# Eight columns of a transposed x copied by DVE in each step, and the scatter product one step behind, in a graph layer on one core

## The chip, the cores and the metric

The kernel runs on one core of one Trainium2 chip. The metric is the device time of one execution in microseconds (us); each run gives one such time, and runs of this kernel lie within about half a per cent of each other. Engines are named as in the profile: PE is the matrix engine (PEld its weight loads), DVE the vector engine, ACT the scalar engine, POOL the engine that issues the indirect gathers, SP the engine that does nothing here but issue DMAs and read registers for their addresses.

## The reference

One layer of a message-passing network over 12,500 nodes (64 features) and 200,000 edges. Edges are sorted by `dst`; `src` is random.

```python
nodes = node_state[edges].reshape(num_edges, -1)          # x[src], x[dst]: 128 features an edge
gates = ssp(edge_state @ We1 + be1) @ We2 + be2           # ssp(v) = softplus(v) - log 2
gates = gates * (1.0 - sigmoid(5.0 * (edges_distance - 3.5)))
h = ssp(nodes @ Wn1 + bn1) @ Wn2 + bn2
message_sum = zeros_like(node_state).at[edges[:, 1]].add(h * gates)
new_state = node_state + (ssp(message_sum @ Ws1 + bs1) @ Ws2 + bs2)
out = layernorm(x + new_state)
```

Half of the input of `nodes @ Wn1` is a row of x for each edge's `src`, so 200,000 random rows of 256 bytes have to be brought in. The other half and the sum over `dst` touch few nodes at a time, since the edges are sorted.

## The kernel before

The edges are cut into 391 groups (`NG`) of 512. A group is four **slots** of 128 edges (`K = 4`), one edge to a partition in tile `xg` (128 x 4 x 128): columns 0 to 63 of a slot take x[src], columns 64 to 105 a one-hot row that says which of 42 neighbouring nodes (`W = 42`) the edge's `dst` is.

x[src] comes in two ways. Most slots are gathered by POOL, one indirect DMA to a slot (`gather`, L231), into a ring of `AHEAD + BEHIND = 19` tiles `xg`; a gather into a used tile waits until the group that had the tile has been through its scatter product. 47 slots are fetched row by row instead (`fetch`, L257): SP issues 7 and ACT 9 direct DMAs of 256 bytes in each step, at addresses that they have read into registers (L245), so that in some groups POOL has three slots or two in place of four.

A loop in Python (L632) writes out the order of the instructions on each engine, one step to a group, with the layers of neighbouring groups interleaved. In step i:

- POOL gathers group i+14; SP loads the edge features and weights of group i+5 (`load`, L278 and L286).
- PE transposes the four slots of group i+1 (L307, into `tx`), and ACT copies the result to SBUF (`xcopy`, L314).
- PE adds biases (L319, L354), and then does the **scatter product** of group i-2 (`scatter`, L383): messages (128 edges x 128) times the one-hot rows, into 84 free columns of the PSUM tile `z` of group i+1. `behind_by` (L624) chooses the group: i-2 up to 12 steps before the end (`CLOSE`), both i-2 and i-1 at that step, and i-1 after it.
- PE does the first layer of group i+1 (L324 for the edge half, L330 for the node half, which waits for `xcopy`); ACT takes exp and log of it (L341, L344), with three row DMAs issued before, between and after them.
- DVE adds the scatter product to the running sums at the place of the group's first node (`window`, L400, two additions, each at an address in a register that DVE has read at L391).
- PE does the second layer of group i (L361, L366, into `gh`); DVE multiplies it by the cutoff (`hcut`, L375) and by the gate (`message`, L379), finishes the softplus of group i+1 (L349), and makes the one-hot rows of group i+3 (L293).
- In some steps there are pieces of the 25 node blocks of the last layer (L419 to L479), which follow when all edges of a block are summed.

Before the loop a table x @ Wn1[64:] + bn1 is made and written to HBM (L591 to L595). Each engine runs its own instructions in this order; between engines there are semaphores.

Of the kernel before, what the change touches and what calls it, by code (L numbers as in the profile page):

```python
# [42 lines left out]
F32 = mybir.dt.float32  # L43
BF16 = mybir.dt.bfloat16
I32 = mybir.dt.int32
# [12 lines left out]
P = 128  # L58
D = 64
# [8 lines left out]
LOADS = 5  # L68
SPREADS = 5
PREPARE = 5  # L70
BEHIND = 5
CLOSE = 12


BLOCK_STEPS = ((2, 3, 4, 4, 6, 7, 8, 9, 10, 14), (2, 3, 3, 4, 5, 6, 7, 8, 9, 10), (1, 2, 1, 2, 3))
# [2 lines left out]
ROWS_FROM = -1  # L78
READY = (5, 7)
LANDED = 4  # L80
CUTOFF = 5.0
EPS = 1e-5
LN2 = 0.6931471805599453
# [3 lines left out]
def node_blocks(N):  # L87

    first = N % NB
    assert N > NB and first % 2 == 0 and first <= HE  # L90
    sizes = ([first] if first else []) + [NB] * (N // NB)
    return [(sum(sizes[:i]), n) for i, n in enumerate(sizes)]


def block_steps(N, NG):

    steps = []
    for at, n in node_blocks(N):
        share = sqrt(min(1.0, (at + n) / N))
        spread = sqrt(share * (1.0 - share) / (NG * GE))  # L100
        steps.append(ceil(NG * (share + SPREADS * spread)))
    return steps


def slots_by_rows(NG):

    slots = []
    for queue in range(2):
        n = 0
        for g in range(READY[queue], NG - 2):  # L110
            if (g - READY[queue] - ROWS_FROM + 1) * ROWS[queue] >= (n + 1) * P:
                slots.append((queue, g, K - 1 - queue))
                n += 1
    return slots


def row_columns(NG):
# [6 lines left out]
def gnn_resnorm_kernel(ctx: ExitStack, tc: tile.TileContext, a: dict, out: bass.AP, E: int):  # L124
# [57 lines left out]
    be3 = const.tile([PIECES, 2, D], BF16, name="be3")  # L182
    row3 = const.tile([PIECES, 2, K, D], BF16, name="row3")
    rs3 = const.tile([PIECES, K, D], BF16, name="rs3")
    wns = const.tile([DW, REST, 2, 2 * D], F32, name="wns")

    xgs, xrs, eTs = {}, {}, {}
# [30 lines left out]
    def padding(g, k):  # L218
        return g * GE + k % 2 * HE + k // 2 * P >= E

    def gather(g):

        xg = loads.tile([P, K, P], F32, name="xg", bufs=AHEAD + BEHIND)
        xgs[g] = xg
        for k in range(K):
            if (g, k) in by_rows:
                continue
            if padding(g, k):
                nc.vector.memset(xg[:, k, :D], 0.0)
                continue  # L230
            note(("gather", g), nc.gpsimd.indirect_dma_start(  # L231
                out=xg[:, k, :D], out_offset=None, in_=x,
                in_offset=bass.IndirectOffsetOnAxis(ap=src_i[:, g, k : k + 1], axis=0)))
# [4 lines left out]
    def read_rows(i, queue, count):  # L238

        count = min(count, rows_left(queue))  # L240
        while i >= ROWS_FROM and len(row_at[queue]) < count:
            q, p = divmod(fetched[queue] + len(row_at[queue]), READ * P)
            assert p % READ == 0
            at = queue * columns_of[0] + q * READ
            row_at[queue] += nc.values_load_multi_w_load_instructions(  # L245
                rows_i[p // READ : p // READ + 1, at : at + READ], engines=[queues[queue].engine], min_val=0,
                max_val=4 * D * (N - 1), skip_runtime_bounds_check_because="src holds rows of x")[1]
# [23 lines left out]
    bases = {}  # L271

    def load(g):
        old = ("scatter", g - LOADS - 4)
        if g % 2 == 0:
            n = min(2, NG - g)
            both = loads.tile([P, 2, HE], F32, name="eT", bufs=4)
            behind(note(("load", g), nc.sync.dma_start(both[:, :n], a["eT"][:, g : g + n, :])), old)  # L278
            for j in range(n):
                eTs[g + j] = both[:, j]  # L280
            _, at = nc.values_load_multi_w_load_instructions(
                base_i[32:33, 2 * g : 2 * g + 4], engines=[SP], min_val=0, max_val=8 * D * (N - 1),
                skip_runtime_bounds_check_because="they were clamped to these bounds")
            bases[g], bases[g + 1] = at[:2], at[2:]
        for h in range(2):
            behind(note(("load", g), nc.sync.dma_start(  # L286
                wns[D:DW, g % REST, h, :].bitcast(U8),
                table_bytes[:, bass.ds(bases[g][h], 8 * D * W)].rearrange("o (w f) -> (o w) f", w=W))), old)

    xTs, zs, us, ss, ghs, hs, msgs, scs = ({} for _ in range(8))  # L290

# [35 lines left out]
    def layer1_node(g):  # L327
        for h in range(2):
            zn = zs[g][:, h, HE * (1 - h) : HE * (2 - h)]
            nc.tensor.matmul(zn, wns[:, g % REST, h, :], xTs[g][:, h], start=True, stop=True,  # L330
                             skip_group_check=True)

    def z_of(g):
        return zs[g].rearrange("p b e -> p (b e)")[:, : 3 * HE]
# [155 lines left out]
    with tc.manual_schedule():  # L490
# [4 lines left out]
        with tc.tile_pool(name="prep", bufs=1) as prep:  # L495
# [11 lines left out]
            for i in range(3):  # L507
                load_x(i)
            nc.sync.dma_start(rows_i, a["rows"])
            dist = cut.rearrange("p g k -> p (g k)")  # L510
            nc.sync.dma_start(dist, a["dist_l"])
            dst_i = rel.bitcast(I32)
# [2 lines left out]
            for g in range(AHEAD):  # L515
# [12 lines left out]
            nc.scalar.dma_start(consts[:, FIRST:], a["consts"][:, FIRST:])  # L528
            nc.scalar.dma_start(wns[:D].rearrange("f r h o -> f (r h) o"),
                                a["Wn1"][:D, :].rearrange("f (r o) -> f r o", r=1).to_broadcast([D, 2 * REST, 2 * D]))  # L530

            dst_f = dst_h.bitcast(F32)
            nc.vector.tensor_copy(dst_f, dst_h)
# [52 lines left out]
            for i in range(PARTS):  # L586
                for c in range(i * CP, (i + 1) * CP, CP // 2):
                    m = CP // 2
                    ps = z_tile().rearrange("p b (k f) -> p (b k) f", k=K)
                    for k in range(m):  # L590
                        nc.tensor.matmul(ps[:, k, :], xT[:, c + k, :], wnb, start=True, stop=True)  # L591
                    tb = prep.tile([P, m, 2 * D], F32, name="tb", bufs=6)
                    nc.scalar.copy(tb[:, :K, :], ps[:, :K, :])
                    nc.vector.tensor_copy(tb[:, K:, :], ps[:, K:m, :])
                    nc.sync.dma_start(by_node[:, c : c + m], tb)  # L595
                    nc.vector.memset(sums[:, c * P : WIDE if c + m == NCH else (c + m) * P], 0.0)
                if i == 1:
                    nc.vector.tensor_copy(base_i[:1], base_b[:1])
                    nc.vector.tensor_scalar(base_i[32:33], base_b[32:33], float(8 * D), None, OP.mult)
                    nc.vector.tensor_scalar(rows_i, rows_i, float(4 * D), None, OP.mult)  # L600
                    for k in range(2):
                        nc.vector.tensor_copy(be3[:, k, :], rows[:, 0, :])
                    for k in range(K):
                        nc.vector.tensor_copy(row3[:, :, k, :], rows[:, 1:3, :])
                        nc.vector.tensor_copy(rs3[:, k, :], rows[:, 3, :])
                if i == 2:
                    nc.scalar.activation(dist, dist, AF.Sigmoid, bias=steep, scale=-5.0)
                    nc.scalar.preload_act_table_set("natural_log_exp_and_others")
                    nc.vector.tensor_copy(rel, dst_i)
                    for t in range(2):  # L610
                        r = rel[:, :, 2 * t : 2 * t + 2]
                        nc.vector.tensor_sub(r, r, base_b[:, :NH].rearrange("p (g h) -> p g h", h=2))


        with tc.tile_pool(name="finish", bufs=1) as finish:
            blocks = list(zip(node_blocks(N), block_steps(N, NG)))
            last = NG - 1
            parts, begun, complete, rest = {}, None, 0, []

            def at(f, g, *more):  # L620
                if 0 <= g < NG:
                    f(g, *more)

            def behind_by(i):  # L624
                close = last - CLOSE
                return [g for g in ([i - 2] if i <= close else []) + ([i - 1] if i >= close else []) if g >= 0]

            for g in range(LOADS - 1):
                load(g)
# [2 lines left out]
            for i in range(-1, last - 1):  # L632
                now = parts.pop(i, [])
                early = [part for part in now if part.tensor]
                at(load, i + LOADS)
                read_rows(i, 0, ROWS[0])
                fetch(i, 0, ROWS[0])
                if i >= 0:
# [4 lines left out]
                fetch(i, 1, ROWS[1] - 6)  # L643
                layer1_bias(i + 1)
                at(layer2_bias, i)
                for n, g in enumerate(behind_by(i)):
                    scatter(g, zs[i + 1][:, 1, HE + 2 * n * W : HE + 2 * (n + 1) * W])
                layer1_edge(i + 1)
                layer1_node(i + 1)
                exps(i + 1)  # L650
                fetch(i, 1, 3)
                logs(i + 1)
                fetch(i, 1, 3)
                for g in behind_by(i):
                    window(g)
                at(layer2, i)
                for part in early:
                    part.tensor(tx_tile())
# [3 lines left out]
                for part in early:  # L662
                    part.others()
                at(onehot, i + 3)
                for part in now:
                    if not part.tensor:
                        part.others()
# [132 lines left out]
def layouts(inputs):  # L800
# [22 lines left out]
    for queue, columns in enumerate(row_columns(NG)):  # L823
        chosen = [out["src_l"].reshape(P, NG, K)[:, g, k] for q, g, k in slots_by_rows(NG) if q == queue]
        v = padded(np.concatenate(chosen), P * columns, 0).reshape(-1, P, READ)
        rows.append(v.transpose(1, 0, 2).reshape(P, columns))
    out["rows"] = np.ascontiguousarray(np.concatenate(rows, axis=1))
    out["dst_l"] = lanes(dst, dst[-1])
    out["dist_l"] = lanes(dist, 1e6)
    out["dst_h"] = np.ascontiguousarray(padded(dst, NR * P * HE, dst[-1]).reshape(NR, P, HE).transpose(1, 0, 2))  # L830
# [42 lines left out]
```

## Time and profile before

| | |
|---|---|
| median of 3 runs | 2684.91 us (2674.76 to 2686.47) |
| the profiled execution: its time, its span | 2686.47 us, 2684.7 us |
| mean granted PE clock | 0.815 of full speed |
| PE / PEld busy | 84% / 65% of the span |
| DVE / ACT / POOL busy | 39% / 36% / 54% |
| instructions on PE / DVE / ACT / POOL | 11373 / 2767 / 1318 / 1520 |
| first L330 / last L330 | 144.1 us / 2661.8 us from the start |
| moved by DMA | 143.53 MB, 53 GB/s on average |

The span runs from the first to the last instruction; 1.8 us of the execution lie outside it. "Busy" leaves out what a sequencer does by itself: reading registers, issuing DMAs, waiting. The recorded ends of matmuls are modelled, so what PE has finished is read better from who starts because of it. The granted clock switches between full and half speed in stretches of some 3 to 27 us all through the loop.

### The profile page before, as it was taken

To read this page: it belongs to the slowest core of one execution; us is meant where nothing else is said; L and a number is where in the kernel's file an instruction comes from. 1 tells how busy PE (TensorE), PEld (TensorE's weight loads), DVE (VectorE), ACT (ScalarE), POOL (GpSimd) and SP (SyncE) were. 2 spreads that over 40 slices of the span, in tenths; PEclk is the share of its full clock that TensorE was granted. 3 is DMA by queue.
4 is the path that set the end of the run, shared out by engine and by line. 5 is a ranking of instruction groups with operands and counts; after the bars stand their busy time and mean duration, and the time that the engine had idled before them with its cause. 6 is when DMAs were issued, how large, how long until landed. Compare 5 with 4: busy or idle time off the path is not lost.

```text
span 2684.7 us, 47845 instructions
## 1 busy us (share of the span) xinstructions
PE 2243.6 (84%) x11373; PEld 1754.9 (65%) x11373; DVE 1052.4 (39%) x2767; ACT 969.6 (36%) x1318; POOL 1441.8 (54%) x1520
## 2 busy tenths in 40 slices
PE   2489888988888888888889788888888888888897
PEld 1467666766666666666667666666666667666676
DVE  1233333333334333344333443434433443444445
ACT  0133333333333333333333333333334333333344
POOL 7335555555555555555555555555555555555520
PEclk9987788788788778788777888778878887787878
DMA  6222222222222212222222222222222222222210
GB/s 159 82 64 52 48 51 49 48 49 48 49 52 50 49 47 51 51 52 47 52 46 50 51 49 53 53 50 53 51 50 50 50 58 48 54 52 50 52 44 25
DMA packets 150911, 143.53 MB, mean 53 GB/s; under 512 B 51887, under 2 KB 98395, under 8 KB 150626
## 3 DMA queue, kind: packets, MB, share of 16 engines
q1 hardware_dynamic: 94090, 88.26, 11.6%
q0 software_dynamic: 48512, 49.77, 9.5%
q10 hardware_dynamic: 8024, 2.37, 0.4%
q8 instruction: 97, 1.59, 0.2%
q14 instruction: 188, 1.54, 0.2%
HBM read 130.59 MB, written 9.63 MB: 52 GB/s over the span
## 4 chain that ended last, share of the span: by engine, by line
PE 64%; another core or an unknown queue 11%; ACTq 10%; ACT 7%; issue 5%; DVE 1%; DMA 0%; DVEq 0%; SPq 0%
PE z L330 16%; PE gh L366 12%; PE z L383 10%; ACTq L257 10%; PE gh L361 7%; PE tx L307 6%; ACT xT L314 6%; PE z L324 4%; PE gh L354 3%; PE z L319 2%; PE tx L419 1%; PE z L591 1%; ACTq L245 1%; PE tx L450 1%
## 5 line engine op out<-in xcount | busy, mean ns | idle before, releaser
L231 POOL DMA_INDIRECT xg<-in_x,src_i x1516 | 1441.6, 951 | 1144.8 <-PE z L383 353.1
L330 PE MATMUL z<-xT,wns 106*128 106x256 f32 x1564 | 574.1, 503 | 322.9 <-ACT xT L314 309.5
L330 PEld LDWEIGHTS z<-xT,wns 106*128 106x128 f32 x1564 | 361.3, 246 | 486.6 <-ACT xT L314 407.9
L341 ACT ACTIVATE u<-z 128x768 f32<-128x768 f32 x392 | 317.4, 810 | 830.4 <-issue 362.4
L366 PE MATMUL gh<-consts,s 128*128 128x64 f32 x3128 | 493.1, 313 | 0.0
L400 DVE TENSOR_TENSOR sums<-sums,z 64x42 f32 x778 | 153.0, 197 | 863.4 <-issue 626.8
L366 PEld LDWEIGHTS gh<-consts,s 128*128 128x128 f32 x3128 | 490.2, 238 | 0.1
L314 ACT COPY xT<-tx 106x512 f32<-106x512 f32 x391 | 228.9, 586 | 670.9 <-remote 231.5
L375 DVE TENSOR_TENSOR h<-gh,cut 128x256 f32<-128x256 f32 x391 | 166.1, 425 | 618.2 <-PE z L383 239.7
L344 ACT ACTIVATE u<-u,one 128x768 f32<-128x768 f32 x392 | 365.9, 934 | 69.7 <-issue 53.3
L349 DVE SCALAR_TENSOR_TENSOR s<-u,z 128x768 f32<-128x768 f32 x392 | 369.4, 943 | 11.1 <-ACT u L344 9.8
L361 PEld LDWEIGHTS gh<-consts,s 128*128 128x128 f32 x1564 | 304.0, 247 | 70.1 <-DVE s L349 32.8
L383 PEld LDWEIGHTS z<-xg,msg 128*128 128x128 f32 x1556 | 240.3, 221 | 152.8 <-issue 148.5
L361 PE MATMUL gh<-consts,s 128*128 128x128 f32 x1564 | 313.8, 335 | 1.8 <-DVE s L349 1.8
L383 PE MATMUL z<-xg,msg 128*128 128x84 f32 x1556 | 306.2, 327 | 0.9 <-DVE msg L379 0.2
L324 PE MATMUL z<-eT,consts 128*128 128x256 f32 x782 | 295.4, 465 | 0.0
L307 PE MATMUL tx<-consts,xg 128*106 128x128 f32 x1517 | 278.6, 312 | 6.4 <-DMA wns<-table 6.4
L307 PEld LDWEIGHTS tx<-consts,xg 128*106 128x106 f32 x1517 | 216.0, 169 | 10.6 <-issue 8.0
L379 DVE TENSOR_TENSOR msg<-gh,h 128x256 f32<-128x256 f32 x391 | 166.0, 425 | 13.4
L354 PE MATMUL gh<-row,ones 3*128 3x512 bf16 x391 | 170.0, 435 | 0.0
L324 PEld LDWEIGHTS z<-eT,consts 128*128 128x128 f32 x782 | 141.7, 226 | 1.2 <-issue 1.2
L293 DVE TENSOR_TENSOR xg<-consts,rel 128x168 f32<-128x168 f32 x391 | 129.9, 332 | 0.0
(93 smaller groups left out, 609.5 us busy)
## 6 DMA issues: line engine op xcount, KB each, us to landing
xr<-in_x ACTq DMA_DIRECT2D x3328, 0.2 KB
eT<-in_eT SPq DMA_DIRECT2D x195, 256.0 KB
xr<-in_x SPq DMA_DIRECT2D x2688, 0.2 KB
xg<-in_x,src_i POOLq DMA_INDIRECT x1516
wns<-table SPq DMA_DIRECT2D x782, 21.0 KB
table<-tb SPq DMA_DIRECT2D x14, 448.0 KB
sums<-in_xT SPq DMA_DIRECT2D x7, 455.0 KB
y<-in_x SPq DMA_DIRECT2D x24, 128.0 KB
```

The costliest lines, as they stand in the source:

```text
L231: note(("gather", g), nc.gpsimd.indirect_dma_start(out=xg[:, k, :D], out_offset=None, in_=x, in_offset=bass.IndirectOffsetOnAxis(ap=src_i[ ...
L257: ins = queues[queue].dma_start(row_tiles[n, "in"][r : r + 1, :D].bitcast(U8), x_bytes[:, bass.ds(row_at[queue].pop(0), 4 * D)])
L307: ins = nc.tensor.transpose(tx[:, k, :], xgs[g][:, k, :DW], ident)
L314: note(("xcopy", g), nc.scalar.copy(xT, xTs[g]))
L324: nc.tensor.matmul(zs[g][:, 0, :HE], we1.rearrange("a h d -> a (h d)"), eTs[g], start=False, stop=True, skip_group_check=True)
L330: nc.tensor.matmul(zn, wns[:, g % REST, h, :], xTs[g][:, h], start=True, stop=True, skip_group_check=True)
L341: nc.scalar.activation(us[g][:, part], z_of(g)[:, part], AF.Exp)
L344: nc.scalar.activation(us[g][:, part], us[g][:, part], AF.Ln, bias=one)
L349: nc.vector.scalar_tensor_tensor(ss[g].rearrange("p i t e -> p (i t e)")[:, part], us[g][:, part], BIG, z_of(g)[:, part], OP.min, OP.max)
L361: nc.tensor.matmul(v[:, 0, t], ss[g][:, 0, t, :], we2, start=False, stop=False, skip_group_check=True)
L366: nc.tensor.matmul(ghs[g][:, 1, 2 * t + h, :], ss[g][:, 1 + h, t, :], wn2, start=False, stop=h == 1 and t == 1, skip_group_check=True)
L383: ins = nc.tensor.matmul(sc, msgs[g][:, 2 * t : 2 * t + 2, :].rearrange("p h f -> p (h f)"), xgs[g][:, 2 * t : 2 * t + 2, D:DW], start=t = ...
```

## The change

Two things are changed together.

**The scatter product.** `behind_by` and `CLOSE` go. In every step the product of group i-1 is made, and added to the sums, in place of that of group i-2. `BEHIND` goes from 5 to 4, so the ring of `xg` has 18 tiles. The condition on `load` moves along: it waits for the scatter of group g-8 in place of g-9, which is the same step.

**The columns.** 23 slots, all with k = 1 (`slots_by_columns`), are no longer gathered by POOL; their columns 0 to 63 of `xg` are set to zero by DVE. The two halves of x lie transposed in SBUF, 64 partitions each, in a tile `xh` of 128 x 6250 float32 (3.2 MB, loaded by SP in four parts in steps 0 to 3). From step 8 on, after the one-hot rows, DVE reads eight indices from SBUF into registers and copies eight columns of `xh` (128 x 1 each) into a tile `column`. 16 steps make one slot, 368 steps all of them. When a slot is full, one instruction sets to zero the half of each column that is another node's (`sides`, `border`), and PE adds Wn1[:64], stacked twice, times that tile to the group's first layer: one 128 x 128 product more in 23 steps. All four transposes of such a group stay.

```diff
-BEHIND = 5
-CLOSE = 12
+BEHIND = 4
+COLUMNS = 8
+COLUMNS_FROM = 8
+XH_PARTS = 4
...
-            if padding(g, k):
+            if padding(g, k) or (g, k) in by_columns:
                 nc.vector.memset(xg[:, k, :D], 0.0)
                 continue
...
+    def columns(i, pool):
+        n = columns_done[0]
+        if i < COLUMNS_FROM or n >= len(by_columns) * P:
+            return
+        p, q = (n // COLUMNS) % P, n // (COLUMNS * P) * COLUMNS
+        _, at = nc.values_load_multi_w_load_instructions(
+            columns_i[p : p + 1, q : q + COLUMNS], engines=[DVE], min_val=0, max_val=half_n - 1,
+            skip_runtime_bounds_check_because="src holds rows of x")
+        slot = list(by_columns)[n // P]
+        if n % P == 0:
+            column_tiles[slot] = pool.tile([P, P], F32, name="column", bufs=2)
+        for j in range(COLUMNS):
+            nc.vector.tensor_copy(column_tiles[slot][:, n % P + j : n % P + j + 1], xh[:, bass.ds(at[j], 1)])
+        columns_done[0] += COLUMNS
+        if columns_done[0] % P == 0:
+            chosen_columns[slot] = pool.tile([P, P], F32, name="chosen", bufs=2)
+            nc.vector.scalar_tensor_tensor(chosen_columns[slot], sides[:, n // P * P : (n // P + 1) * P], border,
+                                           column_tiles[slot], OP.is_ge, OP.mult)
...
+            for t in chosen:
+                nc.tensor.matmul(zn[:, t * P : (t + 1) * P], wn1_twice, chosen_columns[g, 2 * t + h], start=False,
+                                 stop=True, skip_group_check=True)
...
+            nc.sync.dma_start(columns_i, a["columns"])
+            nc.sync.dma_start(sides_i, a["sides"].partition_broadcast(P))
...
+                if 0 <= i < XH_PARTS:
+                    part = slice(half_n * i // XH_PARTS, half_n * (i + 1) // XH_PARTS)
+                    nc.sync.dma_start(xh[:, part], a["xh"][:, part])
...
-                for n, g in enumerate(behind_by(i)):
-                    scatter(g, zs[i + 1][:, 1, HE + 2 * n * W : HE + 2 * (n + 1) * W])
+                if i >= 1:
+                    scatter(i - 1, zs[i + 1][:, 1, HE : HE + 2 * W])
...
-                for g in behind_by(i):
-                    window(g)
+                at(window, i - 1)
...
                 at(onehot, i + 3)
+                columns(i, finish)
```

Ahead of the loop there are also two small loads of Wn1, four DVE instructions that split the indices into a half and a place in it, and a load of 1.5 MB (`sides`, one row sent to all partitions).

More of the change, by code (lines that the diff above doesn't have):

```diff
@@ L114, in slots_by_rows, with slots_by_columns, column_columns @@
     return slots
+def slots_by_columns(NG):
+    slots = []
+    for g in range(NG - 2):
+        if (g - 3 - COLUMNS_FROM + 1) * COLUMNS >= (len(slots) + 1) * P:
+            slots.append((g, 1))
+    return slots
+def column_columns(NG):
+    return -(-len(slots_by_columns(NG)) // COLUMNS) * COLUMNS
 def row_columns(NG):
@@ L184, in gnn_resnorm_kernel @@
     rs3 = const.tile([PIECES, K, D], BF16, name="rs3")
+    half_n = a["xh"].shape[1]
+    by_columns = {slot: n for n, slot in enumerate(slots_by_columns(NG))}
+    columns_i = const.tile([P, column_columns(NG)], I32, name="columns_i")
+    sides_i = const.tile([P, len(by_columns) * P], I32, name="sides_i")
+    sides = sides_i.bitcast(F32)
+    sign = const.tile([P, 1], F32, name="sign")
+    border = const.tile([P, 1], F32, name="border")
+    wn1_twice = const.tile([P, 2 * D], F32, name="wn1_twice")
     wns = const.tile([DW, REST, 2, 2 * D], F32, name="wns")
@@ L273, in load @@
     def load(g):
-        old = ("scatter", g - LOADS - 4)
+        old = ("scatter", g - LOADS - 3)
         if g % 2 == 0:
@@ L288, in load @@
                 table_bytes[:, bass.ds(bases[g][h], 8 * D * W)].rearrange("o (w f) -> (o w) f", w=W))), old)
+    column_tiles, chosen_columns, columns_done = {}, {}, [0]
+    def columns(i, pool):
[16 more added lines that the diff above has]
+                                           column_tiles[slot], OP.is_ge, OP.mult)
     xTs, zs, us, ss, ghs, hs, msgs, scs = ({} for _ in range(8))
@@ L329, in layer1_node @@
             zn = zs[g][:, h, HE * (1 - h) : HE * (2 - h)]
-            nc.tensor.matmul(zn, wns[:, g % REST, h, :], xTs[g][:, h], start=True, stop=True,
+            chosen = [t for t in range(2) if (g, 2 * t + h) in by_columns]
+            nc.tensor.matmul(zn, wns[:, g % REST, h, :], xTs[g][:, h], start=True, stop=not chosen,
                              skip_group_check=True)
+            for t in chosen:
+                nc.tensor.matmul(zn[:, t * P : (t + 1) * P], wn1_twice, chosen_columns[g, 2 * t + h], start=False,
+                                 stop=True, skip_group_check=True)
     def z_of(g):
@@ L530, in gnn_resnorm_kernel @@
                                 a["Wn1"][:D, :].rearrange("f (r o) -> f r o", r=1).to_broadcast([D, 2 * REST, 2 * D]))
+            for h in range(2):
+                nc.scalar.dma_start(wn1_twice[h * D : (h + 1) * D, :], a["Wn1"][:D, :])
+                nc.vector.memset(sign[h * D : (h + 1) * D], 2.0 * h - 1.0)
+                nc.vector.memset(border[h * D : (h + 1) * D], float(half_n if h else 1 - half_n))
             dst_f = dst_h.bitcast(F32)
@@ L600, in gnn_resnorm_kernel @@
                     nc.vector.tensor_scalar(rows_i, rows_i, float(4 * D), None, OP.mult)
+                    upper = prep.tile([P, column_columns(NG)], F32, name="upper")
+                    nc.vector.tensor_scalar(upper, columns_i, float(half_n), float(-half_n), OP.is_ge, OP.mult)
+                    nc.vector.tensor_tensor(columns_i, columns_i, upper, OP.add)
+                    nc.vector.tensor_scalar(sides, sides_i, sign, None, OP.mult)
                     for k in range(2):
@@ L615, in gnn_resnorm_kernel @@
         with tc.tile_pool(name="finish", bufs=1) as finish:
+            xh = finish.tile([P, half_n], F32, name="xh")
             blocks = list(zip(node_blocks(N), block_steps(N, NG)))
@@ L622, in at @@
                     f(g, *more)
-            def behind_by(i):
-                close = last - CLOSE
-                return [g for g in ([i - 2] if i <= close else []) + ([i - 1] if i >= close else []) if g >= 0]
             for g in range(LOADS - 1):
@@ L827, in layouts @@
     out["rows"] = np.ascontiguousarray(np.concatenate(rows, axis=1))
+    chosen = np.concatenate([out["src_l"].reshape(P, NG, K)[:, g, k] for g, k in slots_by_columns(NG)])
+    out["sides"] = np.ascontiguousarray(chosen)
+    v = padded(chosen, P * column_columns(NG), 0).reshape(-1, P, COLUMNS)
+    out["columns"] = np.ascontiguousarray(v.transpose(1, 0, 2).reshape(P, -1))
+    half_n = -(-N // 2)
+    out["xh"] = np.ascontiguousarray(np.concatenate([x[:half_n].T, padded(x[half_n:], half_n, 0.0).T]))
     out["dst_l"] = lanes(dst, dst[-1])
```

## The prediction

> **What bounds the kernel now.** The 40 slices come first: PE 8 to 9 tenths, POOL 5, DVE 3, and PEclk between 7 and 8. That looks like PE. A window view of a stretch in the loop, of one near the end, and of one at half clock says otherwise:
>
> ```profile
> 1526.00:1539.00 13.00, 8.91 (x56) 6.62 (x56) 4.64 (x14) 5.18 (x9) 7.62 (x8) 1.00 0.23 58
> 2596.00:2608.00 12.00, 12.00 (x84) 10.04 (x83) 6.71 (x19) 6.46 (x10) 0.00 (x0) 1.00 0.14 36
> 1400.00:1418.00 18.00, 18.00 (x64) 14.41 (x64) 5.03 (x13) 5.08 (x7) 8.43 (x9) 0.50 0.19 48
> ```
>
> Columns: stretch, its length, then PE, PEld, DVE, ACT and POOL busy, the clock, DMA. At full clock and with gathers running, PE is busy 8.91 of 13 us, and a step takes 6.3 us. After POOL's last gather (2586.9) PE is busy all the time and a step takes 4.09. The work of PE alone would need only that much at full clock. What makes up the rest is seen in the timeline of one period (start, us, engine, line, [idle before <-releaser]):
>
> ```profile
> 1526.56 0.99 POOL L231 DMA_INDIRECT xg<-in_x,src_i  x1 [1.47 <-DVE s L349]
> ...
> 1528.30 1.00 PE L366 MATMUL gh<-consts,s 128*128 128x64 f32 x8
> ...
> 1530.10 0.67 PE L383 MATMUL z<-xg,msg 128*128 128x84 f32 x4
> ...
> 1530.36 0.95 POOL L231 DMA_INDIRECT xg<-in_x,src_i  x1 [0.30 <-issue]
> ...
> 1532.53 0.43 DVE L375 TENSOR_TENSOR h<-gh,cut 128x256 f32<-128x256 f32 x1 [2.95 <-remote]
> ...
> 1532.93 0.95 POOL L231 DMA_INDIRECT xg<-in_x,src_i  x1 [1.63 <-remote]
> 1532.99 0.42 DVE L379 TENSOR_TENSOR msg<-gh,h 128x256 f32<-128x256 f32 x1
> ```
>
> L366 has its last matmul at 1529.3, and `hcut` (L375), which needs nothing else, starts at 1532.53. The scatter product L383 ends at 1530.8, and POOL, which needs it for its next group, starts at 1532.93. The last gather of the group started at 1530.36 and lands some 2.1 us later, at 1532.5. Put over the whole trace: `hcut` is late by over 0.3 us behind L366 in 87% of the steps, `xcopy` behind L307 in 85%, and such a late start comes a median of 29 ns after a gather lands (455 ns for times drawn at random). After the last gather nothing is late. So while POOL gathers, results of PE are seen when a gather lands. POOL's period, from a group's first gather (call it T0) to the next group's, is then three starts 1.25 apart, a landing of 2.1 and some 0.4: 6.2. Counted: 6.28 for four gathers at full clock (128 periods), 7.77 at half clock (56), 6.38 where the clock changes (109). The group of gathers and the scatter product that releases the next one are the bound; PE waits inside of it.
>
> **Gathers removed.** 23 slots leave POOL, 1516 to 1493 gathers. Groups of four take 6.60 on average, of three 5.82, so 0.78 each: 23 x 0.78 = -18. No more than one start, 1.25, can go: -29. No less than 0, if PE sets these steps at half clock. I take -18.
>
> **The scatter product one step later in its data.** This is the large term. `scatter(i-2)` finds its message a step old; `scatter(i-1)` needs the message that DVE makes at this time. Behind the start of `hcut`: .43 + .42 and gaps to the end of L379 = .93; the product .68 at full clock and 1.15 at half; then .26 until POOL begins: POOL is let go 1.9 to 2.4 us behind `hcut`. The ring of 18 tiles in place of 19 doesn't move the step in which POOL waits (it waits for the scatter of its group less 18, in place of less 19), it moves what that product itself waits for. `hcut` starts at T0 + 4.44 in the median at full clock (quartiles 3.91 and 5.86; 5.87 at half clock, 5.77 mixed), at one landing or the next. I took for each counted period the larger of the old one and `hcut` + 1.95 (full), 2.1 (mixed) or 2.35 (half): the mean addition is .65, .84 and .31, over 344 periods .66.
>
> That count assumes that each period keeps its `hcut` where it was; a longer pause of POOL lets some results through sooner, and then the addition shrinks. The other measure is the last twelve steps, which already run with the product one behind, and without gathers:
>
> ```profile
> 2636.83 0.43 DVE L375 TENSOR_TENSOR h<-gh,cut 128x256 f32<-128x256 f32 x1
> 2637.29 0.42 DVE L379 TENSOR_TENSOR msg<-gh,h 128x256 f32<-128x256 f32 x1
> ...
> 2637.76 0.52 PEld L383 LDWEIGHTS z<-xg,msg 128*128 128x128 f32 x4 [0.50 <-DVE msg L379]
> 2637.77 0.68 PE L383 MATMUL z<-xg,msg 128*128 128x84 f32 x4
> ```
>
> PE waits .50 for the message, and a step takes 4.27 in place of 4.09: .18. Between .18 and .66 I take the middle, .42, over the 391 - 12 - 3 = 376 steps that change: +158. Bounds: 0 (a gain has no source: the tile is freed no earlier), and `hcut` always at the last landing, 5.87 + 1.95 = 7.8 against a mean of 6.5, 376 x 1.3 = +490. Behind L383 in PE's queue stand L324 and L330, for which ACT's exp waits, so ACT and then `softplus` come later with it; that is in the .18 and in the count. The later load condition (group less 8) falls in the same step as before; SP's loads run five steps ahead, so nothing is added.
>
> **The columns.** In 368 steps DVE reads eight values, works out addresses and issues eight copies of 128 x 1. Nearest rows: the reading of two values at L391 takes .52, of eight at L245 .73 to .80; an address at L400 .08; small copies start every .10 us:
>
> ```profile
> 110.20 0.17 DVE L604 COPY row<-rows 3x128 bf16<-3x128 bf16 x1
> 110.30 0.16 DVE L605 COPY rs<-rows 3x64 bf16<-3x64 bf16 x1
> 110.39 0.18 DVE L604 COPY row<-rows 3x128 bf16<-3x128 bf16 x1
> ```
>
> Eight copies are .8 to 8 x (.10 + .08) = 1.5 us of DVE's queue, and the reading can go on under `softplus` (.94) and the one-hot rows (.33). Queued behind them are the two additions of `window` and the next `hcut`. Their cover:
>
> ```profile
> L400 DVE TENSOR_TENSOR sums<-sums,z 64x42 f32 x778 | 153.0, 197 | 863.4 <-issue 626.8 <-ACT u L341 230.9 <-DVE sums L400 0.5
> L375 DVE TENSOR_TENSOR h<-gh,cut 128x256 f32<-128x256 f32 x391 | 166.1, 425 | 618.2 <-PE z L383 239.7 <-PE tx L307 184.1 <-remote 96.8
> ```
>
> DVE is idle 863.4 / 389 = 2.2 us a step before L400 and 1.6 before L375: 3.8 against 1.5. I cost the copies at 0, with cover gone 368 x 1.5 = +550; a lengthening of the gathers by them at +10: the 33 gathers that overlap the 128 x 42 copies of L296 take a mean of 975 ns, the 571 that overlap no work of DVE's 946, so .03, and 368 of it is 11.
>
> [...]
>
> **Small terms.** 23 products of 128 x 128 more on PE, .22 at full and .43 at half clock by L361's forms (two passes): 5 to 10, mostly within PE's waits: +4 (0 to 10). 23 instructions `chosen` and 23 of zeroes on DVE: some 10 us under the same idle time, 0. `xh` and `sides`, 4.7 MB, at the 174 GB/s of the first 60 us: 27 us of transfers beside others: +3 (0 to 27). Four tiles of the ring less before the loop, 72 gathers for 76: 0 to -5; I take 0.
>
> **Sum.** 2686.5 - 18 + 158 + 10 + 4 + 3 = 2843.5 for the profiled execution; the median of the runs stands 1.6 lower: **2842**.
>
> **The clock.** It is at full speed in 61% of the loop, and 1.00 in the tail stretch where PE is never idle. PE's longest idle time in the period shown is 2.0 us, and half clock comes all through the loop; I add nothing for it. [...]
>
> **Rivals.**
> *A, forecast: the message stands in POOL's loop*, +.42 a step, chance .57, alone 2730 to 2960. For it: the late `hcut`. Against: the phases may settle anew.
> *B, it costs only what the tail shows*, 376 x .18 = 68 in place of 158: 2752 (2690 to 2765), chance .15. It decides if results pass PE as soon as POOL pauses, so that the group is released at the landing that already sets it.
> *C, faster: the wait is hidden altogether*, and POOL gains a whole start for each slot: 2686.5 - 29 + 10 - 1.6 = 2666, chance .14. One mechanism: where `hcut` starts by T0 + 4.3 in nearly all periods, the product is done by the landing at T0 + 5.9 that POOL waits for anyway. For it: the lower half of `hcut` starts at full clock does so. Against: the upper quartile at 5.86 and the median of 5.87 at half clock.
> *D, the columns become DVE's bound*, or hold POOL: 2842 + 368 x .4 = 2990 for .4 us that the idle time doesn't take up, chance .09. From 3.8 us a step (copies and addresses near .4 each) it decides.
> *E, gain and cost cancel*, 2685, chance .05.
> That the change doesn't remove what it says: the gathers go surely; the transposes of these slots stay, so PE gains nothing.
>
> **Numbers.** 2842; range 2665 to 2960, which leaves out part of C below and of D above, under 2 in 10. Half a per cent, 13.4 us, is what a measurement of this kernel can tell from no change. Faster .14 (C); same .08 (E and .03 of B); slower .78 (A, D and the rest of B).
>
> **What would show it.** L231 with 1493 instructions. For the large term: POOL's period at full clock up from 6.28 to 6.7 with the idle before its groups released at L383 right behind L379, and PEld L383 waiting for `msg` in most steps. For the columns: a group of 2944 copies near .1 to .16 us, with L400's idle time less by about their sum and `hcut` no later behind L366. Wrong it would be if POOL's period stays at 6.3 (C), if DVE has no idle time left before L400 (D), or if the share of half clock moves by a tenth or more.

## The result and the profile after

The changed kernel takes 3074.73 us in the median of four runs (3062.95 to 3080.35), against 2683.74 for the kernel before: a ratio of 1.146, 95% interval 1.141 to 1.150. The forecast was 2842, at most 2960. The sign was right, and the loss is two and a half times the one worked out.

The groups of the profile after (line, engine, operation, names, count | busy us, mean ns | idle before it <-releasers). L231 is now L255, L366 is L416, L375 is L425, L379 is L429, L383 is L433, L400 is L450; L329 are the copies. The first two lines are of the kernel before:

```profile
L231 POOL DMA_INDIRECT xg<-in_x,src_i x1516 | 1441.6, 951 | 1144.8 <-PE z L383 353.1 <-issue 352.1 <-DVE s L349 182.5
L383 PEld LDWEIGHTS z<-xg,msg 128*128 128x128 f32 x1556 | 240.3, 221 | 152.8 <-issue 148.5 <-DVE msg L379 3.6 <-DVE s L349 0.6
```

```profile
L255 POOL DMA_INDIRECT xg<-in_x,src_i x1493 | 1410.6, 945 | 1572.7 <-PE z L433 592.3 <-DVE s L399 452.6 <-issue 352.8
L433 PEld LDWEIGHTS z<-xg,msg 128*128 128x128 f32 x1556 | 273.2, 249 | 776.3 <-DVE msg L429 744.8 <-issue 23.8 <-DVE l_s L484 2.4
L329 DVE COPY column<-xh 128x1 f32 x2944 | 247.3, 147 | 36.8 <-issue 36.1
L425 DVE TENSOR_TENSOR h<-gh,cut 128x256 f32<-128x256 f32 x391 | 166.0, 425 | 791.4 <-remote 380.1 <-PE tx L353 295.5 <-PE gh L416 57.5
L450 DVE TENSOR_TENSOR sums<-sums,z 64x42 f32 x778 | 153.0, 197 | 823.7 <-issue 604.6 <-ACT u L391 213.0 <-ACT l_s L488 0.6
```

POOL has 23 gathers fewer, 31 us less work, and 428 us more idle time: 1572.7 against 1144.8. The difference of the two, 397, is the whole loss (the span grew by 393.9). PE's weight loads wait 744.8 us for messages ahead of the scatter product, where they waited 3.6. DVE, which carries 2944 more instructions, is hardly less idle before L450 (823.7 against 863.4) and more idle before `hcut` (791.4 against 618.2). So DVE has not run out of time, and yet its `hcut` starts later. The timeline of one period shows where (T0 is again the start of a group's first gather):

```profile
1721.22 0.94 POOL L255 DMA_INDIRECT xg<-in_x,src_i  x1 [3.25 <-DVE s L399]
1721.24 0.57 DVE L329 COPY column<-xh 128x1 f32 x8
...
1724.12 1.12 PE L416 MATMUL gh<-consts,s 128*128 128x64 f32 x8
...
1724.97 0.94 POOL L255 DMA_INDIRECT xg<-in_x,src_i  x1 [0.30 <-issue]
1727.17 0.42 DVE L425 TENSOR_TENSOR h<-gh,cut 128x256 f32<-128x256 f32 x1 [2.42 <-PE tx L353]
...
1727.63 0.42 DVE L429 TENSOR_TENSOR msg<-gh,h 128x256 f32<-128x256 f32 x1
1728.11 0.93 PEld L433 LDWEIGHTS z<-xg,msg 128*128 128x128 f32 x4 [2.40 <-DVE msg L429]
...
1729.53 0.94 POOL L255 DMA_INDIRECT xg<-in_x,src_i  x1 [3.62 <-PE z L433]
```

T0 is 1721.22. L416 ends at 1725.2, the fourth gather, started at 1724.97, lands at 1727.1, `hcut` follows at T0 + 5.95, and from there the chain of the prediction runs as priced: message, product, POOL's next group, 2.36 us behind `hcut`, a period of 8.31. Between 250 and 2450 us, `hcut` starts at T0 + 5.83 in the median of the 17 groups of four gathers that run at full clock throughout (quartiles 5.79 and 5.89), where the kernel before has 4.44 in 120 such groups (3.77 and 5.86).

### The profile page after: what moved, and what is told of

It is laid out like the page before. It is cut to its first block, busy times and chain, and to the rows that moved or that the text cites. A ratio compares the mean times of both kernels' runs of the same rounds, so it can differ in the third digit from the quotient of the medians.

```text
span 3078.6 us, 53961 instructions
## 1 busy us (share of the span) xinstructions
PE 2333.5 (76%) x11419; PEld 1918.8 (62%) x11419; DVE 1281.9 (42%) x5764; ACT 968.7 (31%) x1318; POOL 1410.8 (46%) x1497
## 4 chain that ended last, share of the span: by engine, by line
PE 53%; DVE 15%; another core or an unknown queue 15%; issue 10%; DVEq 4%; ACT 1%; ACTq 1%; DMA 0%; SPq 0%
PE z L377 13%; PE gh L416 10%; PE z L433 8%; PE tx L353 7%; PE z L370 6%; PE gh L411 6%; DVE h L425 5%; DVE msg L429 4%; DVEq L322 2%; DVE column L329 2%; DVE sums L450 1%; DVE s L399 1%; DVEq L441 1%; ACTq L281 1%
## 5 line engine op out<-in xcount | busy, mean ns | idle before, releaser
L255 POOL DMA_INDIRECT xg<-in_x,src_i x1493 | 1410.6, 945 | 1572.7 <-PE z L433 592.3
L433 PE MATMUL z<-xg,msg 128*128 128x84 f32 x1556 | 345.6, 359 | 615.3 <-DVE msg L429 600.7
L433 PEld LDWEIGHTS z<-xg,msg 128*128 128x128 f32 x1556 | 273.2, 249 | 776.3 <-DVE msg L429 744.8
L377 PE MATMUL z<-xT,wns 106*128 106x256 f32 x1564 | 616.4, 537 | 18.3 <-ACT xT L360 13.6
L377 PEld LDWEIGHTS z<-xT,wns 106*128 106x128 f32 x1564 | 430.4, 277 | 126.1 <-ACT xT L360 23.7
L450 DVE TENSOR_TENSOR sums<-sums,z 64x42 f32 x778 | 153.0, 197 | 823.7 <-issue 604.6
L425 DVE TENSOR_TENSOR h<-gh,cut 128x256 f32<-128x256 f32 x391 | 166.0, 425 | 791.4 <-remote 380.1
L416 PEld LDWEIGHTS gh<-consts,s 128*128 128x128 f32 x3128 | 494.4, 240 | 0.0
L416 PE MATMUL gh<-consts,s 128*128 128x64 f32 x3128 | 490.8, 312 | 0.0
L411 PEld LDWEIGHTS gh<-consts,s 128*128 128x128 f32 x1564 | 343.1, 271 | 49.9 <-DVE s L399 2.0
L370 PE MATMUL z<-eT,consts 128*128 128x256 f32 x782 | 350.5, 541 | 0.0
L411 PE MATMUL gh<-consts,s 128*128 128x128 f32 x1564 | 331.7, 352 | 1.7 <-DVE s L399 1.7
L329 DVE COPY column<-xh 128x1 f32 x2944 | 247.3, 147 | 36.8 <-issue 36.1
L429 DVE TENSOR_TENSOR msg<-gh,h 128x256 f32<-128x256 f32 x391 | 165.9, 424 | 13.4
L370 PEld LDWEIGHTS z<-eT,consts 128*128 128x128 f32 x782 | 164.9, 261 | 0.6 <-issue 0.6
```

What stands on the lines that cost most here:

```text
L255: note(("gather", g), nc.gpsimd.indirect_dma_start(out=xg[:, k, :D], out_offset=None, in_=x, in_offset=bass.IndirectOffsetOnAxis(ap=src_i[ ...
L329: nc.vector.tensor_copy(column_tiles[slot][:, n % P + j : n % P + j + 1], xh[:, bass.ds(at[j], 1)])
L370: nc.tensor.matmul(zs[g][:, 0, :HE], we1.rearrange("a h d -> a (h d)"), eTs[g], start=False, stop=True, skip_group_check=True)
L411: nc.tensor.matmul(v[:, 0, t], ss[g][:, 0, t, :], we2, start=False, stop=False, skip_group_check=True)
L416: nc.tensor.matmul(ghs[g][:, 1, 2 * t + h, :], ss[g][:, 1 + h, t, :], wn2, start=False, stop=h == 1 and t == 1, skip_group_check=True)
L425: nc.vector.tensor_mul(hs[g], ghs[g][:, 1], cut[:, g, :].to_broadcast([P, K, D]))
```

## The experiments

The first four runs undid the parts one by one.

```diff
 # one_behind: the kernel before, product one step behind throughout, 18 tiles
-BEHIND = 5
-CLOSE = 12
+BEHIND = 4
+CLOSE = 400
-        old = ("scatter", g - LOADS - 4)
+        old = ("scatter", g - LOADS - 3)
 # one_behind_ring19: CLOSE = 400 alone
 # ring18: BEHIND = 4 alone
 # columns_two_behind: the changed kernel with
-                if i >= 1:
-                    scatter(i - 1, zs[i + 1][:, 1, HE : HE + 2 * W])
+                for n, g in enumerate(behind_by(i)):
+                    scatter(g, zs[i + 1][:, 1, HE + 2 * n * W : HE + 2 * (n + 1) * W])
...
-                at(window, i - 1)
+                for g in behind_by(i):
+                    window(g)
 # and BEHIND = 5, CLOSE = 12, the load condition as before, one buffer for column and for chosen
```

> The kernel before with the scatter product and the additions one step behind in every step, and the ring of 18 tiles; no columns, all 1516 gathers. Theory M (the message stands in POOL's loop, with the layer-two results seen only at the last landing): the changed kernel's trace has groups of four gathers at 7.86 us and groups of three at 6.72, so 23 slots more cost 23 x 1.14 = 26: about 3100 (3070 to 3130), groups of four near 7.9. Rival R1 (the copies of the columns cause a good part of the loss): 2753 to 2842, the two prices forecast for the later product alone. Rival R2 (the ring of 18 tiles causes it): like M here, and separated by the next two runs.

> The kernel before with the product one step behind in every step, the ring kept at 19 tiles. M: POOL always waits for the newest scatter product, whatever the ring's size, so as the run with 18 tiles, within 15 us. R2: back near 2685.

> The kernel before with 18 tiles in place of 19 and nothing else; the product stays two steps behind. M: 2685 within 15. R2: 2900 or more.

> The changed kernel with the product two steps behind as in the kernel before, 19 tiles, one buffer in place of two for the tiles column and chosen. M: the columns give their gathers back: 2685 less 18 to 29 plus up to 10, 2655 to 2680. R1: the copies cost what the changed kernel lost beyond the later product, 2850 to 2950.

The kernel before took 2638.11 there. Measured: **one_behind** 1.055 (1.048 to 1.061), **one_behind_ring19** 1.047 (1.040 to 1.054), **ring18** 1.001 (0.997 to 1.004), **columns_two_behind** 1.003 (0.999 to 1.008). The ring does nothing that these runs can tell. Theory M (the later product alone explains the loss) fell as it was written: 3100 was expected of the later product alone, and it came out at 2776, within R1's 2753 to 2842. R1 (the copies cause a good part of it) fell as it was written too, since the columns alone cost next to nothing. Each part is about as dear as the prediction had it, and together, 1.055 x 1.003 = 1.058, they should have given some 2840; 1.146 was measured. The parts don't add. The profiles of the two halves show why (first one_behind, then columns_two_behind, groups of instructions):

```profile
L231 POOL DMA_INDIRECT xg<-in_x,src_i x1516 | 1436.3, 947 | 1224.1 <-issue 356.2 <-PE z L383 355.9 <-DVE s L349 315.4
L375 DVE TENSOR_TENSOR h<-gh,cut 128x256 f32<-128x256 f32 x391 | 166.1, 425 | 403.3 <-PE tx L307 141.2 <-remote 119.5 <-issue 66.1
```

```profile
L256 POOL DMA_INDIRECT xg<-in_x,src_i x1493 | 1420.2, 951 | 1145.3 <-PE z L434 410.1 <-issue 348.2 <-remote 114.1
L330 DVE COPY column<-xh 128x1 f32 x2944 | 246.2, 145 | 35.8 <-issue 34.8
L426 DVE TENSOR_TENSOR h<-gh,cut 128x256 f32<-128x256 f32 x391 | 166.1, 425 | 722.3 <-PE z L434 271.1 <-PE tx L354 214.4 <-remote 140.7
```

DVE's idle time before `hcut` is the number to read. With the product two steps behind it is 618.2 without columns (the kernel before) and 722.3 with them; one step behind, it is 403.3 without and 791.4 with them (the changed kernel). Two steps behind nobody is in a hurry for the message, so 722.3 costs nothing: POOL idles 1145.3, as before. One step behind, the lateness stands in POOL's loop. Counted over the groups of four gathers between 250 and 2450 us of each trace (hcut's start measured from T0):

```
                      period   hcut median   hcut at T0 + 5.5 or later
before                 6.61       5.21              45%
columns_two_behind     6.62       5.82              86%
one_behind             6.81       4.34              21%
no_column_work_5       7.08       4.53              33%
fixed_columns_4        7.52       5.78              57%
after                  7.88       5.87              80%
```

The last four rows are all one step behind, and their periods rise with the share of late starts; the first two are two steps behind, and the share doesn't matter. (The runs with a number behind their name come further down.) The next question was what in the columns makes `hcut` late. The first three of the next kernels leave out x[src] of the 23 slots, or put other rows in its place:

```diff
 # no_column_work: the changed kernel without the reading and the copies
-        _, at = nc.values_load_multi_w_load_instructions(columns_i[p : p + 1, q : q + COLUMNS], ...
-        for j in range(COLUMNS):
-            nc.vector.tensor_copy(column_tiles[slot][:, n % P + j : n % P + j + 1], xh[:, bass.ds(at[j], 1)])
+        if n % P == 0:
+            nc.vector.memset(column_tiles[slot], 0.0)
 # fixed_columns: without the reading, copies from xh[:, n + j : n + j + 1]
 # reads_only: with the reading, without the copies
 # base_first: ahead of columns(i, finish)
+                if i >= 0 and i not in window_at:
+                    window_bases(i)
```

> The changed kernel without DVE's reading of eight values and without the eight copies of each step (the tile column is set to zero when a slot begins; the 23 slots' x[src] is left out so). All else stays: one behind, 18 tiles, 1493 gathers, the products, the loads. The later product alone came out at 1.055 of before, the columns alone at 1.003, both at 1.146. Theory L (the second register read of DVE, the one for the addresses of window, is queued behind the copies, so that it falls into the time in which gathers hold results up, and hcut goes to the last landing): 1.035 to 1.06. Theory C (the copies themselves do that): 1.035 to 1.06 too. Theory G (it is something else in the change: fewer gathers, the products, the smaller room): 1.12 to 1.15.

> The changed kernel with the eight copies at fixed places of xh, so without DVE's reading of eight values and without addresses (the 23 slots get other rows of x). L: 1.035 to 1.07, hcut at full clock back at T0 + 4.5 or earlier in half of the periods. C: 1.12 to 1.15, hcut at T0 + 5.8.

> The changed kernel with the reading of eight values in each step, and no copies (the 23 slots' x[src] is left out). L: 1.08 to 1.15, since the read for window stands behind the other one. C: 1.035 to 1.06.

> The changed kernel, complete, with the register read for the next step's window put ahead of the reading of the eight values and the copies. L: 1.04 to 1.08, the read for window again right behind the one-hot rows, hcut early again. C: 1.12 to 1.15 as in the changed kernel.

The kernel before took 1939.1 us in these runs, not 2638, and the four, in this order, came out at 0.988 (0.986 to 0.989), 0.988 (0.986 to 0.991), 0.987 (0.985 to 0.988) and 1.002 (1.000 to 1.004). What that is was seen from the changed kernel itself, run with three of them beside it:

> The changed kernel once more, since the four runs before this took place on another chip, on which the kernel before takes 1939 and no result of PE is late. If the kernel before takes some 2640 to 2690 here: 1.13 to 1.16. If it takes some 1940: 0.99 to 1.01 (23 gathers at 1.25 less, and the copies as in the run with the read for window put first, which was at 1.002 there).

> The same kernel as no_column_work, for the same question, beside the changed kernel. Where the kernel before takes 2640 to 2690: theories L and C (register read, copies) 1.035 to 1.06, theory G (something else in the change) 1.12 to 1.15. Where it takes 1940: 0.987.

> The same kernel as fixed_columns. Where the kernel before takes 2640 to 2690: L 1.035 to 1.07, C 1.12 to 1.15. Where it takes 1940: 0.988.

> The same kernel as base_first. Where the kernel before takes 2640 to 2690: L 1.04 to 1.08, C 1.12 to 1.15. Where it takes 1940: 1.002.

The kernel before took 1936.77 here, the changed kernel 1927.22: a ratio of **0.996** (0.994 to 0.998), faster by 0.4%. The other three were at 0.987 (0.985 to 0.989), 0.988 (0.986 to 0.990) and 1.003 (1.001 to 1.005). So all kernels here run under one of two conditions, each of which held for a whole set of runs made together: the kernel before at 2638 to 2685, or at 1937 to 1941. The result and the first four runs are of the first. The recorded number of the chip doesn't tell them apart (number 12 had 2638 in the first set and 1937 in this one). Ratios are compared within one condition only. The page of after_again, the same program as the changed kernel's, has these busy times and this row of the granted clock:

```profile
PE 1757.0 (91%) x11419; PEld 1450.0 (75%) x11419; DVE 1313.0 (68%) x5764; ACT 962.0 (50%) x1318; POOL 1420.8 (74%) x1497
...
PEclk9999999999999999999999999999999999999997
```

Its groups:

```profile
L255 POOL DMA_INDIRECT xg<-in_x,src_i x1493 | 1420.6, 951 | 458.4 <-issue 358.1 <-DMA xg<-in_x,src_i 27.5 <-PE gh L416 10.1
L425 DVE TENSOR_TENSOR h<-gh,cut 128x256 f32<-128x256 f32 x391 | 165.9, 424 | 23.0 <-PE gh L416 9.4 <-issue 0.2
```

The gather is as long as ever, 951 ns, and POOL gathers without a break: of its 458.4 us idle 358.1 are the .30 between gathers. `hcut` waits 23.0 us in all, in place of 791.4, and the mean granted clock is .983, in place of .777. All that the prediction built on, late results and POOL waiting for the product, is of the other condition. The question of the copies could be answered only there.

> The changed kernel without the reading of eight values and the copies. Where the kernel before takes 2640 to 2690 and results of PE are late: theories L and C 1.035 to 1.06, theory G 1.12 to 1.15. Where it takes 1940 again: 0.987, and nothing new on the three theories.

> The changed kernel with copies at fixed places, no reading of eight values. Where the kernel before takes 2640 to 2690: L 1.035 to 1.07 and hcut early in half of the periods, C 1.12 to 1.15 and hcut at the last landing. Where it takes 1940: 0.988.

> The changed kernel with the register read for the next window ahead of the reading of the eight values. Where the kernel before takes 2640 to 2690: L 1.04 to 1.08, C 1.12 to 1.15. Where it takes 1940: 1.002.

The kernel before at 1939.2: 0.988 (0.986 to 0.989), 0.987 (0.985 to 0.989), 1.003 (1.001 to 1.004), which repeats the other condition and tells nothing on the copies.

> The changed kernel with the eight copies of a step at fixed places of xh, without the reading of eight values and without addresses. The changed kernel's own trace speaks against something outside of the columns' work: in its steps 3 to 7, ahead of the first copies, a step takes some 6 us, and 7.4 from step 8 on. Where the kernel before takes 2640 to 2690: if the reading and the addresses keep the results of PE back, 1.035 to 1.07; if the copies do, 1.12 to 1.15. Where it takes 1940: 0.988, and the question stays open.

The kernel before at 2677.38: **1.117** (1.109 to 1.124), and `hcut` at T0 + 5.78 in the median. The copies keep `hcut` late without the reading of values and without addresses. Theory L, which had only the reads at work and expected at most 1.07, falls with it. That the reads add something is not excluded: reads_only and base_first have no run under this condition, and in the trace of columns_two_behind `hcut` is late in some 60% of the groups whose read for `window` lies ahead of T0 + 0.6, and in 95% of those where it lies at T0 + 1.2 to 3.0, with a median of T0 + 5.7 to 5.9 in either case.

> The changed kernel without the reading of eight values and without the copies, all else kept. With copies at fixed places it was at 1.117 where the kernel before takes 2677. Where the kernel before takes 2640 to 2690 here too: if the copies are the cause, 1.035 to 1.06, hcut at full clock in the median before T0 + 4.5; if something else in the change is (fewer gathers, the products, the smaller room), 1.10 to 1.15. Where it takes 1940: 0.987, and this stays open.

The kernel before at 1940.81, and 0.987 (0.985 to 0.989): nothing on this.

> The changed kernel without the reading of eight values and without the copies, all else kept (the 23 slots' x[src] is left out). Where the kernel before takes 2640 to 2690: if the copies are the cause, 1.035 to 1.06, hcut at full clock in the median before T0 + 4.5; if something else in the change is, 1.10 to 1.15. Where it takes 1940: 0.987, and this stays open.

The kernel before at 2683.11: **1.056** (1.049 to 1.062), as one_behind, and `hcut` at T0 + 2.94 in the median at full clock. Whatever else the change brought, fewer gathers, 23 products, 4.7 MB more of loads, the smaller room, is worth nothing beyond the later product that these intervals can tell. The groups of the last two under this condition (no_column_work_5, then fixed_columns_4):

```profile
L255 POOL DMA_INDIRECT xg<-in_x,src_i x1493 | 1409.9, 944 | 1327.9 <-PE z L430 446.2 <-issue 345.3 <-DVE s L396 309.6
L422 DVE TENSOR_TENSOR h<-gh,cut 128x256 f32<-128x256 f32 x391 | 166.1, 425 | 485.7 <-PE tx L350 189.2 <-remote 153.9 <-PE gh L413 72.3
```

```profile
L255 POOL DMA_INDIRECT xg<-in_x,src_i x1493 | 1409.8, 944 | 1472.3 <-PE z L430 487.8 <-DVE s L396 465.5 <-issue 350.4
L326 DVE COPY column<-xh 128x1 f32<-128x1 f32 x2944 | 210.2, 145 | 0.0
L422 DVE TENSOR_TENSOR h<-gh,cut 128x256 f32<-128x256 f32 x391 | 166.1, 425 | 707.1 <-remote 325.8 <-PE tx L350 250.4 <-PE gh L413 67.7
```

Eight copies a step, 210.2 us of an engine that idles, take DVE's idle time before `hcut` from 485.7 to 707.1 and POOL's from 1327.9 to 1472.3. It is not that PE gets its second layer done later: of the groups of four in which its last matmul ends between T0 + 2.25 and T0 + 2.75, `hcut` starts at T0 + 5.5 or later in 19% without the copies (no_column_work_5), in 56% with copies at fixed places and in 83% in the changed kernel. Steps of the loss, one step behind: later product 1.056, copies 1.117 / 1.056 = 1.058, what is left for reading and addresses 1.146 / 1.117 = 1.026. These ratios are of different sets of runs, though of one condition, and each carries some 0.6% either way.

## Why the prediction was wrong

**What bounds the kernel**: POOL's group of gathers and the scatter product that releases the next, under the condition of the runs shown; that held. The reading of what lets PE's results through was half right. It was said that results are seen when a gather lands. For `xcopy` that is so: in the trace before 83% of its late starts lie within 60 ns of a landing, 12% by chance. Late starts of `hcut` go more with something else: 78% come at most .1 us after the end of one of SP's issues of row DMAs (11% by chance), 52% lie within 60 ns of a landing (12% by chance). SP's issues are themselves held up, .71 us at the 95th percentile against .26 in after_again, where `hcut` hardly waits (23.0 us in all). `hcut`'s starts gather at T0 + 3.7, 4.4, 5.1 and 5.9; the first three, which let it through early, lie between the landings at T0 + 3.4, 4.6 and 5.9. That SP and PE are let through together is read from these times; what holds both up is not shown.

**Gathers removed**, -18: where POOL never waits, no_column_work gains 1.2 to 1.3%, some 25 us of 1939, near the upper end of 29; where it waits, the gain is not seen apart. (The trace before has 5.96 for groups of three, not 5.82, so the same sum gives -15.)

**The later product**, .42 a step or +158: the run of it alone gave 5.5% of 2638, 145 us or .38 a step. Mechanism and size were right, the size with some luck, since .42 was only the middle between .18 and .66. In that run `hcut` even came earlier than before, in 21% of the groups at T0 + 5.5 or later in place of 45%, which agrees with the prediction's "a longer pause of POOL lets some results through sooner".

**The columns** with the gathers removed and the small terms, 0 + 10 - 18 + 4 + 3 = -1: alone 1.003 (0.999 to 1.008), some 9 us. Right as well, with the product two steps behind.

**The step that failed** is the sum. It was written "I cost the copies at 0", with DVE's idle time of 3.8 us a step as the cover, and `hcut` was taken for the later product from the trace before, as if the copies did not move it. The prediction named the check itself, "`hcut` no later behind L366", and did not price what a later `hcut` costs once the product stands right behind it. The runs show it in its place: the columns move `hcut` from T0 + 5.21 to 5.82 in the median while the product is two steps behind, and from 4.34 to 5.87 when it is one behind. The prediction's own count (the larger of the old period and `hcut` + 1.95 to 2.35) gives .69 a step in the trace before, and 1.17 in the trace of columns_two_behind: 376 x 1.17 = +440, an estimate, against a measured loss of +391. The bound was in the prediction's text too: always at the last landing, 376 x 1.3 = +490, which gives 2842 - 158 + 490 = 3174. The range stopped at 2960, short of it. Rival D, which had the loss come from the columns, asked for copies and addresses near .4 us each; the copies follow each other at .06 to .11, and it is not DVE's time that runs out.

**The gathers' lengthening by copies**, +.03 each: in the changed kernel the 374 gathers that overlap copies take a mean of 942 ns, the other 1119 take 946. There is no lengthening. The copies do cost 5.8%, but by a later `hcut`; in what way they keep PE's results back was not shown.

**The clock** was given nothing, and fell from .815 to .777. Between 300 and 1700 us PE has 71 idle gaps over 2.0 us (the longest in the period that the prediction shows) in the changed kernel and 25 in the kernel before; the loop is at half clock for 48% of its time in the one and for 39% in the other, so that the share rises far less than the gaps do. In after_again PE is busy for 91% of the span, in place of 76%, at .983. Whether idle gaps bring the half clock was not shown. What the clock adds to the loss was not separated: groups of four gathers take 7.51 at full clock in the changed kernel and 8.36 at half, so the larger part of the loss stands at full clock too (6.30 before).

**Open** are two things. Why eight copies of 128 x 1 on DVE keep PE's results from being seen, in place of letting them through one opening earlier, although no gather gets longer (942 ns beside copies, 946 without); copies by another engine were not run. And what sets the condition: neither the chip's number nor the kernel does.

## What to carry to other kernels

Two edits can cost far more together than the sum of each alone (1.055 and 1.003 here, and 1.146 together): one makes a result late where nobody waits, and the other makes somebody wait for it. Before adding two prices, ask for each start time that the one edit uses whether the other moves it, and price the case in which it goes to its bound. A stage that has an engine idle is no cover for work that changes when that engine is told of a result (DVE idled 3.8 us a step in the kernel before, and eight copies took the ratio from 1.056 to 1.117); look at when its next instruction starts, not at how long it was idle.

## What had not been expected of the hardware

- One program takes 3075 or 1927 us, and the kernel before 2684 or 1937, with the same 53,961 instructions in the changed kernel and the same gather of .95. Its PE clock is .78 in the one and .98 in the other; while gathers run, `hcut` is late (over .3 us behind L416) in 314 of the 361 steps in which DVE waits for it in the one, and in 1 of 13 in the other. The change is a loss of 14.6% in the one and a gain of 0.4% in the other.
- The columns' cost by itself: a copy of 128 x 1 takes 147 ns and starts .06 to .11 behind the one before; reading eight values takes .63 in the median, each address .05. Where the kernel before takes 1937, the change without them is at 0.987 and with them at 0.996.
